# State space layer of a metaformer: decay tiles five turns ahead in eight buffers, one shared copy of B, C and step rows, and the norm's sums, root and scaling four turns later

## Chip, cores and metric

The kernel runs on one core of a Trainium2 chip. The metric is the device time of one execution in microseconds (us). The time before the change is 11213.39 us, the median of 3 runs (11188.75 to 11217.96).

## What is computed

The reference is a network of four layers, each a mixing step and a feed-forward step with residuals. The change touches only the mixing step of the third layer (`L2_conv`), a state space layer (Mamba). Cut to what matters:

```python
x = x + _L2_conv_ref(_ln_c(x), ...)

def _L2_conv_ref(x, ln_g, ln_b, ...):
    xn = (xf - mu) * lax.rsqrt(var + LN_EPS) * ln_g + ln_b      # over d_model
    xm = _mamba(xn, in_proj_w, conv_w, conv_b, x_proj_w, dt_proj_w, dt_proj_b, A_log, D, out_proj_w)
    h1 = gelu(einsum('...w,hw->...h', out, fc1_w) + fc1_b)
    return einsum('...h,oh->...o', h1, fc2_w) + fc2_b

def _mamba(u, ...):
    xi, z = split(einsum('bld,ed->ble', u, in_proj_w))
    xs = silu(causal convolution of xi over l, 4 taps)
    x_dbl = einsum('bld,ed->ble', xs, x_proj_w)
    dt, Bm, Cm = x_dbl[..., :4], x_dbl[..., 4:20], x_dbl[..., 20:]
    dt = softplus(einsum('blr,dr->bld', dt, dt_proj_w) + dt_proj_b)
    A = -exp(A_log)
    def step(h, t):                                   # for every l, 16 states for each of 128 channels
        h = exp(dt_t[:, :, None] * A) * h + (dt_t * x_t)[:, :, None] * B_t[:, None, :]
        y = einsum('bds,bs->bd', h, C_t)
    y = (ys + xs * D) * silu(z)
    return einsum('bld,ed->ble', y, out_proj_w)
```

## The kernel before, in words

The function `l2_conv` does this layer. The sequence is cut into 64 **chunks** of 512 positions for two images each (`b` = 0 and 1). A chunk has 32 **units**, 16 for each image (8 pairs of states times two halves of the channels). One unit sweeps two states of 64 channels as one [128 x 512] tile:

- **decay** (ACT, L2770): `da = exp(dt * A)`, from the tile `dt0` or `dt1` into a tile `da` (5 buffers). It is issued three turns ahead of its unit.
- **spread** (PE, L2780): a matmul that copies the rows of B for two units into a PSUM bank (`bs`); three turns ahead.
- **inputs** (DVE, L2814): `db = dx * bs`, one turn ahead.
- **scan** (DVE, L2822): `hist = scan(da, db)`, the recurrence itself.
- **gs** (POOL, L2827): `hist * C`, with the rows of C fetched by DMA (`cc`); every fourth unit POOL also saves the last column (L2829).
- **summed** (PE, L2838, and L2836 for the term xs * D): adds gs of the states into PSUM, five turns later, two units at a time.

Units 16 and 17 of each chunk are "apart": their da lies in PSUM, and their product is POOL's (L2808).

The order of the work is written by hand. The loop over `t` runs one **turn** per unit; inside a turn every engine gets its instructions in the order decay, spread, fetches, inputs, scan and gs, then the steps that were put down for this turn with `at(turn, ...)`, then summed. The engines take their instructions strictly in this order, so an instruction that waits holds up all that comes later on its engine. Within a turn the steps of `leave` come first, then those of `project`, then those of `norm`.

Four groups of steps feed the units; all turns are counted modulo 32:

- `statistics(n)` serves four chunks at once: DVE takes sums in turns 7 to 22 (L2441), POOL merges them in turn 24 (L2447 to L2453), ACT takes a root in turn 26 (L2457), POOL refines in turn 28 (L2469).
- `norm(n)` prepares the input of a chunk two chunks ahead: `scale` (ACT, L2487, turns 30 and 0), `centre` (PE, L2493, turn 3), `square` (ACT, L2496 and L2497, turn 4), `mean2` (PE, L2502, turn 5), `root` (ACT, L2506 to L2508, turn 6), `newton` (POOL, L2512 to L2515, turn 8), `back` (PE, L2521, turn 11), `kept` (ACT, L2527, turn 12), `done` (POOL, L2534 and L2535, turn 13).
- `project(n)` runs one chunk ahead: the convolution (PE, L2567, turns 24 to 27; ACT, L2579, turn 28), the gate (PE, L2585, turn 30; ACT, L2588), silu (ACT, L2594, turn 1), the rows of B, C and step (PE, L2600, turns 7 and 8), their copies out of PSUM (ACT, L2604 to L2606, turn 9) and corrections for a bf16 remainder (PE, L2615; ACT, L2621; turns 10 to 13), the steps (PE, L2626, turn 15), softplus (ACT, L2630 and L2631 in turn 16, L2634, L2638 and L2639 in turn 17, L2642 in turn 18; POOL, L2645 in turn 18, L2648 in turn 20), `size` (POOL, L2658, turn 21, giving dt) and `scaled` (POOL, L2662, turn 23, giving dx). After each of the last two, SP issues four DMAs (L2654) that lay out dt and dx for the units 0 to 15 of the next chunk; the copies for its other half follow in turns 1 and 2 of that chunk.
- `leave(n)` finishes a chunk: the gating (DVE, L2694, turns 21 and 5), the output product (PE, L2699, turns 9 and 13; ACT, L2702, turns 10 and 14), the two dense layers (PE, L2707, turns 18 and 21; ACT, L2712, turns 19 and 22; GELU, ACT, L2717, turn 24; PE, L2723 to L2726, turns 28 to 32) and the output (ACT, L2733).

In PSUM, the pool `pn` has a single slot for the tiles of centre, mean2, back, the output product and the last layer; `pa` has a single slot for the convolution, the gate, the rows, the steps and the first dense layer. So these follow each other strictly.

The three copies that the change touches are

```python
nc.scalar.copy(tile_of(x_, "bt", [3 * N, 2, L], dt=BF16), ps[0 : 3 * N])
nc.scalar.copy(tile_of(x_, "bc", [2 * N, 2, L], bufs=1), ps[0 : 2 * N])
nc.scalar.copy(tile_of(x_, "r", [R, 2, L], bufs=1), ps[3 * N : 3 * N + R])
```

with N = 32 and R = 4; SP writes `bc[0:N]` to DRAM for the fetches of C, and L2626 multiplies `r` with `dtw`.

Of the kernel before, what the change touches and what calls it, by code (L numbers as in the profile page):

```python
# [10 lines left out]
F32 = mybir.dt.float32  # L11
# [11 lines left out]
P = 128  # L23
# [2278 lines left out]
def l2_conv(env, x, out, prm):  # L2302
# [15 lines left out]
    with ExitStack() as ctx:  # L2318
# [65 lines left out]
        nc.vector.tensor_scalar(minus_i, env.ident[0 : 2 * N, 0 : 2 * N], -1.0, None, ALU.mult)  # L2384
        both = cp.tile([P, H], F32, name="both")
        nc.vector.tensor_add(both, env.ident[:, 0:H], env.ident[:, H:P])
        dtw = load("dtw", [R, D], prm["dt_proj_wT"])
        dtb = load("dtb", [P, 1], prm["dt_proj_b"].unsqueeze(1))
        am = cp.tile([P, S // 2, 2], F32, name="am")
        for i in range(2):  # L2390
# [27 lines left out]
        def at(turn, *steps):  # L2418
            turns.setdefault(turn, []).extend(steps)
# [58 lines left out]
        def norm(n, t0):  # L2478
            g, w0 = chunks[n]
            x_ = boxes[n]  # L2480

            def scale(js):
                r, k = x_["rows"]
                if 0 in js:
                    tile_of(x_, "xn", [P, 3 + L], bufs=3)
                for j in js:
                    nc.scalar.activation(  # L2487
                        x_["xn"][:, 3 + j * C : 3 + j * C + C], r["xt"][:, k + j, :], AF.Identity,
                        bias=r["nb"][:, k + j : k + j + 1], scale=r["rs16"][:, k + j : k + j + 1],
                    )  # L2490

            def centre():
                nc.tensor.matmul(tile_of(x_, "pm", [P, L], "pn", 1, pool=p1), less, x_["xn"][:, 3:], start=True, stop=True)  # L2493

            def square():
                nc.scalar.copy(x_["xn"][:, 3:], x_["pm"])  # L2496
                nc.scalar.activation(tile_of(x_, "sq", [P, L], "sq", 1), x_["pm"], AF.Square)  # L2497

            def mean2():
                pv = tile_of(x_, "pv", [P, NW, 2], "pn", 1, pool=p1)  # L2500
                for q in range(NW):
                    nc.tensor.matmul(pv[:, q, :], x_["sq"][:, q * C : q * C + C], each, start=True, stop=True)  # L2502

            def root():
                v, rs = tile_of(x_, "v", [P, NW, 2]), tile_of(x_, "rs", [P, NW, 2])
                nc.scalar.activation(v, x_["pv"], AF.Identity, bias=env.eps5)  # L2506
                nc.scalar.activation(rs, v, AF.Ln)
                nc.scalar.activation(rs, rs, AF.Exp, scale=-0.5)  # L2508

            def newton():  # L2510
                v, rs, t = x_["v"], x_["rs"], tile_of(x_, "r2", [P, NW, 2])
                nc.gpsimd.tensor_tensor(t, rs, rs, ALU.mult)  # L2512
                nc.gpsimd.tensor_tensor(t, t, v, ALU.mult)
                nc.gpsimd.tensor_scalar(t, t, 0.5, -1.5, ALU.mult, ALU.add)
                nc.gpsimd.tensor_tensor(rs, rs, t, ALU.mult)  # L2515

            def back():
                pr = tile_of(x_, "pr", [P, L], "pn", 1, pool=p1)
                for q in range(NW):
                    for b in range(2):  # L2520
                        nc.tensor.matmul(  # L2521
                            pr[b * H : b * H + H, q * C : q * C + C], x_["rs"][:, q, b : b + 1].to_broadcast([P, H]),
                            env.ident, start=True, stop=True,
                        )

            def kept():
                nc.scalar.copy(tile_of(x_, "rt", [P, L], bufs=1), x_["pr"])  # L2527

            def done():
                xn = x_["xn"]  # L2530
                if w0 == 0:
                    nc.gpsimd.memset(xn[:, 0:3], 0.0)
                else:
                    nc.gpsimd.tensor_copy(xn[:, 0:3], boxes[n - 1]["xn"][:, L : L + 3])  # L2534
                nc.gpsimd.tensor_tensor(xn[:, 3:], xn[:, 3:], x_["rt"], ALU.mult)  # L2535

            at(t0 - 2, lambda: scale((0, 1)))
            at(t0, lambda: scale((2, 3)))
            at(t0 + 3, centre)
            at(t0 + 4, square)  # L2540
            at(t0 + 5, mean2)
            at(t0 + 6, root)
            at(t0 + 8, newton)
            at(t0 + 11, back)
            at(t0 + 12, kept)
            at(t0 + 13, done)


        def project(n, t0):
# [52 lines left out]
            def bcr_out():  # L2602
                ps = x_["ps"]
                nc.scalar.copy(tile_of(x_, "bt", [3 * N, 2, L], dt=BF16), ps[0 : 3 * N])  # L2604
                nc.scalar.copy(tile_of(x_, "bc", [2 * N, 2, L], bufs=1), ps[0 : 2 * N])
                nc.scalar.copy(tile_of(x_, "r", [R, 2, L], bufs=1), ps[3 * N : 3 * N + R])  # L2606

            def c_out():
                for b in range(2):
# [13 lines left out]
            def steps():  # L2623
                pu = tile_of(x_, "pu", [P, 2, L], "pa", 1, pool=pa)
                for b in range(2):
                    nc.tensor.matmul(pu[:, b, :], dtw, x_["r"][:, b, :], start=True, stop=True)  # L2626

            def parts():
                pu = x_["pu"]
# [58 lines left out]
        def leave(n, t0):  # L2688
# [48 lines left out]

            at(t0 - S + LAG, lambda: sums(0))
            at(t0 + LAG, lambda: sums(1))
            at(t0 + 9, lambda: project_out(0))  # L2740
            at(t0 + 10, lambda: projected(0))
            at(t0 + 13, lambda: project_out(1))
            at(t0 + 14, lambda: projected(1))
            at(t0 + 18, lambda: layer1(0))
# [21 lines left out]

        def decay(t):
            x_, b, s, _ = unit(t)
            da = bank(t, t % 2) if apart(t) else sb.tile([P, L], F32, name="da", bufs=5)
            nc.scalar.activation(da, x_["dt%d" % b][:, s % 2, :], AF.Exp, scale=am[:, s : s + 1])  # L2770
            live["da", t] = da

# [72 lines left out]
        with tc.manual_schedule(engines={E_.PE, E_.Activation, E_.DVE, E_.Pool}):  # L2845
            base_table()
            for n in range(0, len(chunks), NG):
                statistics(n, T * (n - 3))
            for n in range(len(chunks)):
                norm(n, T * (n - 2))  # L2850
                project(n, T * (n - 1))
                leave(n, T * (n + 1))
            for t in range(-4 * T, units + 2 * T):
                if 0 <= t + 3 < units:
                    decay(t + 3)
                if 0 <= t + 3 < units:
                    if (t + 3) % 2 == 0 and not apart(t + 3):
                        spread(t + 3)
                if 0 <= t + 10 < units and t % 2 == 0 and apart(t + 10):
                    fetch_b(t + 10)  # L2860
                if 0 <= t + 5 < units and apart(t + 5):
                    inputs_apart(t + 5)
                if t % QU == 2 and 0 <= t + 6 < units:
                    fetch(t + 6)
                if 0 <= t + 1 < units and not apart(t + 1):
                    inputs(t + 1)
                if 0 <= t < units:
                    one_state(t)
                for step in turns.pop(t, ()):
                    step()  # L2870
                if 0 <= t - LAG < units and (t - LAG) % 2 == 1:
                    summed(t - LAG)
# [697 lines left out]
```

## Time and profile before

| | |
|---|---|
| median of 3 runs | 11213.39 us (11188.75 to 11217.96) |
| the profiled execution, own time | 11202.36 us |
| its span, first to last instruction | 11200.5 us |
| the state space layer's units, first to last scan | 6334.0 to 10199.3 us |
| 6330 to 10200 us, busy: DVE, POOL, PE, ACT | 3694.5, 3510.1, 3382.7, 3178.2 of 3870 us |
| granted clock of PE in that stretch | 0.89 |
| mean duration of scan (L2822), input product (L2814) | 1271 ns, 677 ns |
| mean duration of gs (L2827), decay (L2770) | 1273 ns, 715 ns |

A line of the groups reads: line, engine, operation, output and inputs, shapes, count, then busy time and mean ns of one, then the engine's idle time just before these instructions and what ended it. Consecutive instructions of DVE overlap by about 0.1 us, so that a scan and its product take 1.77 us together. A line of the table of waits reads: who waited, for whom, us in total, times, longest. A line of a timeline reads: start, duration, engine, line, operation, operands, and in brackets the idle time before it and what ended it. "PEld" is PE's weight load.

### The profile page before, as it was taken

To read this page: it belongs to the slowest core of one execution; us is meant where nothing else is said; L and a number is where in the kernel's file an instruction comes from. 1 tells how busy PE (TensorE), PEld (TensorE's weight loads), DVE (VectorE), ACT (ScalarE), POOL (GpSimd) and SP (SyncE) were. 2 spreads that over 40 slices of the span, in tenths; PEclk is the share of its full clock that TensorE was granted. 3 is DMA by queue.
4 is the path that set the end of the run, shared out by engine and by line. 5 is a ranking of instruction groups with operands and counts; after the bars stand their busy time and mean duration, and the time that the engine had idled before them with its cause. 6 is when DMAs were issued, how large, how long until landed. Compare 5 with 4: busy or idle time off the path is not lost. (4 is left out here: it accounts for less than half of the span.)

```text
span 11200.5 us, 114412 instructions
## 1 busy us (share of the span) xinstructions
PE 6448.2 (58%) x33010; PEld 3781.1 (34%) x33010; DVE 9431.5 (84%) x14943; ACT 7408.7 (66%) x10451; POOL 5992.4 (54%) x5674
## 2 busy tenths in 40 slices
PE   7777686000000000003999688888888888887665
PEld 5665454000000000002898333333333333334342
DVE  7567646999999999998778599999999999997455
ACT  4244443788886777765555488888888888885443
POOL 1000025899992000001455499999999999894222
PEclk8887798555555555556999789889988989898877
DMA  6312246111111111112111254554554545543534
GB/s 195 107 36 48 56 160 159 51 58 56 59 58 54 57 54 56 53 45 61 47 56 47 70 126 119 127 126 118 131 123 121 128 122 123 129 116 108 193 132 169
DMA packets 806489, 1080.31 MB, mean 96 GB/s; under 512 B 245612, under 2 KB 462927, under 8 KB 792271
## 3 DMA queue, kind: packets, MB, share of 16 engines
q1 hardware_dynamic: 761918, 946.59, 30.6%
q0 software_dynamic: 34368, 124.14, 3.3%
q8 instruction: 266, 4.36, 0.2%
q14 instruction: 385, 3.15, 0.1%
q10 hardware_dynamic: 9552, 2.08, 0.1%
HBM read 699.16 MB, written 255.91 MB: 85 GB/s over the span
## 5 line engine op out<-in xcount | busy, mean ns | idle before, releaser
L2827 POOL TENSOR_TENSOR gs<-hist,cc 128x512 f32<-128x512 f32 x2048 | 2570.8, 1273 | 268.5 <-DVE hist L2822 200.9
L2822 DVE TENSOR_TENSOR_SCAN hist<-da,state,bs 128x512 f32<-128x512 f32 x1860 | 2360.0, 1271 | 48.2 <-ACT da L2770 47.0
L1698 PE MATMUL pm<-ident,m 128*1 128x128 f32 x1 | 0.4, 372 | 3193.0 <-DVE m L1696 3193.0
L2814 DVE TENSOR_TENSOR bs<-dx,bs 128x512 f32<-128x512 f32 x1920 | 1299.3, 677 | 159.9 <-PE bs L2780 110.9
L1506 POOL TENSOR_TENSOR diff<-key 128x2048 f32<-128x2048 f32 (+11 forms) x364 | 1384.0, 3851 | 81.8 <-DVE key L1511 75.5
L2770 ACT ACTIVATE da<-dt,am 128x512 f32<-128x512 f32 x1920 | 1294.5, 715 | 38.2 <-DVE hist L2822 29.7
L2838 PE MATMUL py<-gs,both 128*64 128x512 f32 x4096 | 1212.9, 672 | 1.4 <-POOL gs L2827 1.3
L1698 PEld LDWEIGHTS pm<-ident,m 128*1 128x1 f32 x1 | 0.1, 79 | 3193.1 <-issue 3193.1
L1936 POOL IOTA row<- 72x1 int32 x1 | 0.2, 230 | 1770.4 <-ACTq L1873 1770.4
L1528 ACT COPY keep<-rank 128x1536 int16<-128x1536 int16 (+11 forms) x364 | 612.8, 1686 | 437.7 <-DVE rank L1530 389.0
L1504 ACT COPY low<-key 128x2048 f32<-128x2048 f32 (+11 forms) x364 | 627.7, 1725 | 313.6 <-DVE key L1511 276.5
L1529 DVE COPY_PREDICATED rank<-back,rank 128x1536 int16<-128x1536 uint8 (+11 forms) x364 | 781.7, 2147 | 16.7 <-ACT keep L1528 16.7
L1530 DVE COPY_PREDICATED rank<-back,keep 128x1536 int16<-128x1536 uint8 (+11 forms) x364 | 777.8, 2137 | 12.5
L1511 DVE TENSOR_TENSOR key<-low,key 128x2048 f32<-128x2048 f32 (+11 forms) x364 | 744.5, 2045 | 12.4
L1510 DVE TENSOR_TENSOR key<-low,key 128x2048 f32<-128x2048 f32 (+11 forms) x364 | 749.1, 2058 | 2.4 <-ACT low L1504 2.4
L1507 ACT ACTIVATE turned<-diff 128x2048 int8<-128x2048 f32 (+11 forms) x364 | 600.4, 1699 | 8.4 <-POOL diff L1506 8.4
L1519 ACT ACTIVATE back<-turned 128x3072 uint8<-128x3072 int8 (+12 forms) x182 | 582.5, 3200 | 0.0
L2249 PE MATMUL pe<-ew,xg 128*128 128x128 f32 x4096 | 506.6, 278 | 0.0
L2249 PEld LDWEIGHTS pe<-ew,xg 128*128 128x128 f32 x4096 | 491.0, 193 | 19.2 <-issue 2.9
L1031 POOL DMA_DIRECT2D state<-zz x16 | 18.5, 1156 | 856.2 <-DVE zz L1021 615.8
L2780 PE MATMUL bs<-bt,pick 96*128 96x512 bf16 x960 | 394.5, 411 | 120.0 <-DVE hist L2822 117.5
L2707 PE MATMUL pa<-o,f 128*128 128x256 f32 x1024 | 361.5, 514 | 107.5 <-ACT gl L2712 93.4
(858 smaller groups left out, 17618.0 us busy)
## 6 DMA issues: line engine op xcount, KB each, us to landing
cc<-cd SPq DMA_DIRECT2D x1024, 256.0 KB
xt<-state SPq DMA_DIRECT2D x64, 1024.0 KB
dt<-w SPq DMA_DIRECT2D x512, 128.0 KB
dx<-up SPq DMA_DIRECT2D x512, 128.0 KB
xo<-state SPq DMA_DIRECT2D x128, 256.0 KB
state<-xo POOLq DMA_DIRECT2D x128, 256.0 KB, 3.0
xl<-in_L_ffn_weight SPq DMA_DIRECT2D x32, 1024.0 KB
tk<-in_x SPq DMA_DIRECT2D x32, 512.0 KB
```

Source lines behind the costliest of these rows:

```text
L1504: nc.scalar.copy(c, l)
L1506: nc.gpsimd.tensor_sub(d, lo[part], hi[part])
L1510: nc.vector.tensor_tensor(lo[part], c, hi[part], ALU.min)
L1511: nc.vector.tensor_tensor(hi[part], c, hi[part], ALU.max)
L1529: nc.vector.copy_predicated(l, t, h)
L1530: nc.vector.copy_predicated(h, t, kv)
L2249: T.matmul(w["pe"][:, j, :], w["xg"][:, q, j, :], ew[:, q, :], start=False, stop=(j == 3 and q == E - 1))
L2770: nc.scalar.activation(da, x_["dt%d" % b][:, s % 2, :], AF.Exp, scale=am[:, s : s + 1])
L2814: nc.vector.tensor_mul(live["db", t], x_["dx%d" % b][:, s % 2, :], live["bs", t - s % 2])
L2822: nc.vector.tensor_tensor_scan(h, live.pop(("da", t)), live.pop(("db", t)), 0.0 if first else state[b][:, s : s + 1], ALU.mult, ALU.add,)
L2827: nc.gpsimd.tensor_tensor(gs, h, live.pop(("cc", t)), ALU.mult)
L2838: nc.tensor.matmul(x_["py%d" % b][h * H : h * H + H], both, live.pop(("gs", t - 1 + h)), start=False, stop=(s == S - 1),)
```

## The change

The decay of every unit that is not apart is issued five turns ahead instead of three, and `da` has eight buffers instead of five. The copy `r` is dropped: one copy takes all 100 rows of B, C and step, and the matrix `dtw` becomes [100 x 128], zero but for its last four rows, so that the steps' matmul reads the shared tile with 100 rows instead of 4. In `norm`, square moves by one turn, mean2, root, newton, back and kept by four, done by five. In `leave`, the first output product and its copy move from turns 9 and 10 to 11 and 12.

```diff
-        dtw = load("dtw", [R, D], prm["dt_proj_wT"])
+        dtw = cp.tile([3 * N + R, D], F32, name="dtw")
+        nc.vector.memset(dtw, 0.0)
+        nc.sync.dma_start(dtw[3 * N :], prm["dt_proj_wT"])
...
             at(t0 + 3, centre)
-            at(t0 + 4, square)
-            at(t0 + 5, mean2)
-            at(t0 + 6, root)
-            at(t0 + 8, newton)
-            at(t0 + 11, back)
-            at(t0 + 12, kept)
-            at(t0 + 13, done)
+            at(t0 + 5, square)
+            at(t0 + 9, mean2)
+            at(t0 + 10, root)
+            at(t0 + 12, newton)
+            at(t0 + 15, back)
+            at(t0 + 16, kept)
+            at(t0 + 18, done)
...
-                nc.scalar.copy(tile_of(x_, "bc", [2 * N, 2, L], bufs=1), ps[0 : 2 * N])
-                nc.scalar.copy(tile_of(x_, "r", [R, 2, L], bufs=1), ps[3 * N : 3 * N + R])
+                nc.scalar.copy(tile_of(x_, "bc", [3 * N + R, 2, L], bufs=1), ps[0 : 3 * N + R])
...
-                    nc.tensor.matmul(pu[:, b, :], dtw, x_["r"][:, b, :], start=True, stop=True)
+                    nc.tensor.matmul(pu[:, b, :], dtw, x_["bc"][:, b, :], start=True, stop=True)
...
-            at(t0 + 9, lambda: project_out(0))
-            at(t0 + 10, lambda: projected(0))
+            at(t0 + 11, lambda: project_out(0))
+            at(t0 + 12, lambda: projected(0))
...
-            da = bank(t, t % 2) if apart(t) else sb.tile([P, L], F32, name="da", bufs=5)
+            da = bank(t, t % 2) if apart(t) else sb.tile([P, L], F32, name="da", bufs=8)
...
-                if 0 <= t + 3 < units:
+                if 0 <= t + 5 < units and not apart(t + 5):
+                    decay(t + 5)
+                if 0 <= t + 3 < units and apart(t + 3):
                     decay(t + 3)
```

## The prediction

> **What bounds the kernel now.** I read the page first. Its slices give the state space stage (L2827, L2822, L2814, L2770) to slices 22 to 35, with DVE at nine tenths. The groups name the work: 2048 scans and 1920 input products.
>
> ```profile
> L2822 DVE TENSOR_TENSOR_SCAN hist<-da,state,bs 128x512 f32<-128x512 f32 x1860 | 2360.0, 1271 | 48.2 <-ACT da L2770 47.0
> L2814 DVE TENSOR_TENSOR bs<-dx,bs 128x512 f32<-128x512 f32 x1920 | 1299.3, 677 | 159.9 <-PE bs L2780 110.9 <-DMA dx<-up 46.7
> ```
>
> Their last columns are the idle time that any change can win back: 48 + 111 us, beside one start-up wait of 45.3 us inside the 46.7. The table of waits of the stage (6330 to 10200 us) says what stands behind:
>
> ```profile
> PEld pn L2502 <- ACT sq L2497: 224.7, 61, 5.4
> DVE bs L2814 <- PE bs L2780: 110.9, 100, 3.0
> POOL e L2645 <- ACT less L2639: 65.3, 62, 3.0
> ACT rs L2457 <- POOL v L2453: 65.1, 15, 4.4
> PE pa L2615 <- ACT r L2606: 55.0, 63, 1.7
> DVE hist L2822 <- ACT da L2770: 48.0, 54, 3.1
> ```
>
> Sorting DVE's idle gaps by unit of the chunk (scans counted in order): the da waits lie before unit 5 (40.9 us, of which 32.5 in every fourth chunk, where the statistics of the next four end) and unit 30 (6.1). The waits for PE lie at scans 9 (25.7), 21 (28.4), 25 (41.6) and 1 to 3 (11.3).
>
> The waits that DVE has are half of it. A join that costs nothing yet shows only in the timelines. POOL in one chunk:
>
> ```profile
> 8781.14 1.08 POOL L2535 TENSOR_TENSOR xn<-xn,rt 128x512 f32<-128x512 f32 x1
> ...
> 8788.88 2.36 POOL L2645 TENSOR_TENSOR e<-e,less 128x1024 f32<-128x1024 f32 x1 [0.38 <-ACT less L2639]
> 8791.19 1.27 POOL L2827 TENSOR_TENSOR gs<-hist,cc 128x512 f32<-128x512 f32 x1
> ...
> 8793.77 2.36 POOL L2648 TENSOR_TENSOR up<-up,e 128x1024 f32<-128x1024 f32 x1
> ...
> 8797.31 2.37 POOL L2658 TENSOR_TENSOR w<-w,up 128x1024 f32<-128x1024 f32 x1
> ...
> 8802.22 2.39 POOL L2662 TENSOR_TENSOR up<-w,xs 128x1024 f32<-128x1024 f32 x1
> ```
>
> and DVE, whose line is the next chunk's first product, with no idle before it:
>
> ```profile
> 8809.03 0.67 DVE L2814 TENSOR_TENSOR bs<-dx,bs 128x512 f32<-128x512 f32 x1
> ```
>
> From L2645 to the end of L2662 (8804.61) POOL never rests. Then four DMAs copy dx; the trace's semaphore updates put the last landing 4.15 us later, at 8808.75. DVE starts 0.28 us after that. Over the chunks this slack is mostly 0.2 to 0.6 us (1.2 in the chunk with statistics). So a chunk has two halves, each with its own limit: from the scan of unit 15 to this product (mean of 56 chunks 29.47 us), where POOL's chain is level with DVE, and from there to the next unit 15 (31.08 us), where DVE runs with gaps. 64 x 60.55 = 3875 us, the stage.
>
> **The change, part by part.** The sum is made against the profiled execution: span 11200.5, its own time 11202.4; the median of the runs, 11213.4, is 11 us above.
>
> 1. *Norm's scaling to turn 18.* L2534 and L2535 now follow L2645 on POOL, at the head of the chain above: 1.20 us from start to start (8780.99 to 8782.19). Everything to the landing of dx is late by it. Where they stood, POOL only waited for ACT afterwards (1.0 us a chunk), so nothing comes back. Queued behind them: gs of units 19 to 23, the three big products, SP's copies of dt and dx, and the merge of the statistics (L2453), for which ACT waits.
> 2. *kept (L2527) to turn 16.* It runs behind L2631 and ahead of the decay, L2634, L2638 and L2639, which POOL awaits. Its 0.583 us count as 0.49 between starts. It delays the chain too. Its old place, turn 12, had room.
> 3. *One copy fewer (L2606).* 63 x 1.007 = 63 us leave ACT, and PE's 55 us wait at L2615 goes. Both lie before L2626, and L2626 stands behind the spread of unit 18, which needs scan 14. That start is a floor: 0.3 us after scan 15 begins, reached now in chunks with statistics, against 0.97 in the others. L2626 itself with 100 rows instead of 4: L2567 with 64 rows takes 628 ns, L2600 with 128 rows 680, L2626 652 now: 0 taken, -0.1 to +0.1 us a chunk. The wider copy: 1005 ns for 64 partitions and 1007 for 4, so nothing. The memset and the DMA of dtw stand in the set-up, once, at most one 128x512 DVE product, 0.7 us.
> 4. *Root and sums later (mean2 5 to 9, root 6 to 10, newton, back 11 to 15).* PE's wait at L2502 goes (ACT has four turns for the square), and with it DVE's 25.7 us at scan 9 and a few tenths around it. In its place PE waits for L2694 before L2836 (1.98 us in the last chunk, which has no norm), without a spread behind it that is due. back, 1.09 us, comes after L2626 and hides beside L2630 and L2631 (2.0 us). The output products moved from 9 and 10 to 11 and 12 keep PSUM's single slot in order: one turn between neighbours, as before.
> 5. *Eight da tiles, five turns ahead.* ACT gains two units, 3.5 us, before DVE misses a da: the 48 us of da waits go, the longest being 3.1. The price is the first decay of a chunk, which wants dt two turns sooner. dt lands 4.2 us after L2658, and the third decay behind GELU comes 22.0 us after L2630, so ACT waits some tenths where it has idle time (1 to 1.8 us at L2733 next).
>
> *PE's clock.* With the waits of 3 and 4 gone and back out of the way, PE idles before the spread of unit 18: I add its work from L2836 on (PE free 15.85 us after scan 5, scan 15 at 17.7) and get 1.9 us. The rows show what that can do. Two timelines, 0.32 and 1.34 us of idle time:
>
> ```profile
> 8780.47 0.38 PE L2780 MATMUL bs<-bt,pick 96*128 96x512 bf16 x1 [0.32 <-DVE hist L2822]
> 8780.78 1.98 PE L2626 MATMUL pa<-r,dtw 4*128 4x512 f32 x4
> ```
>
> ```profile
> 9082.44 0.38 PE L2780 MATMUL bs<-bt,pick 96*128 96x512 bf16 x1 [1.34 <-DVE hist L2822]
> 9082.75 3.07 PE L2626 MATMUL pa<-r,dtw 4*128 4x512 f32 x4
> ```
>
> The same four matmuls take 1.98 and 3.07 us; behind 2.1 and 2.8 us of idle time L2630 follows 3.9 us after their start, not 2.1. Of waits between 1 and 2 us some 4 in 10 slow the matmuls behind them. So L2630 starts 0.3 + 2.1 = 2.4 us after scan 15, or 0.3 + 3.5 = 3.8; half and half, 3.1 (now 3.06, and 2.79 with statistics).
>
> [...]
>
> **The sum, a chunk.** Second half: 3.1 + 5.95 (L2630 to the end of L2639) + 0.49 + 0.08 + 2.36 (L2645) + 1.20 + 13.36 (to the end of L2662) + 4.15 = 30.7, +1.2 on 29.47. DVE's gaps at scans 21 and 25 lie inside this half, so what becomes of them no longer matters.
>
> First half: the lowest seen is 28.9, and 30.45 with statistics, mean 29.3. Three chunks in four come down to it but for 0.1 us. In the fourth ACT waits for POOL's merge, now about 1.6 us later against DVE, and PE waits for ACT (L2585, 1.8 to 2.7 us, then 3.4 or more), runs at half pace, and brings the spreads of units 2 and 4 late. One chunk shows it today (PE gap 2.59, DVE's stall 2.95, no da wait), others show the da wait of 3.05 instead. I put 4.6 for what this chunk keeps of its 4.8. Mean 29.3 + (4.6 + 0.3)/4 = 30.5, -0.6.
>
> Together +0.65 x 63 = +41 us: 11202 + 41 = 11243, which is 30 us (0.3%) above the median of the runs.
>
> **Rivals.**
>
> A. *The join does not lengthen much, nothing won beyond it.* PE stays at full pace, L2630 at 2.4: second half 30.0, first 30.5, together as now: 11200, give or take 25. For it: one of the 1.9 us waits in two. Chance 0.30.
>
> B. *Faster.* As A, and the fourth chunk loses its stall too, because DVE, held at the join, gives ACT time: first half 29.4, -1.15 x 63 = -72: 11130. It decides if PE's wait for L2579 stays under about 2 us. Against it: POOL's merge lies behind the same chain. Chance 0.17.
>
> C. *Slower still: PE cold before L2626 in every chunk.* L2630 at 3.8, and the fourth chunk 1 us worse: 31.4 + 30.8, +1.65 x 63 = +104: 11306. It decides from an idle time of about 2 us before the spread of unit 18. Chance 0.13.
>
> D. *The lead of five turns does not arrive,* since dt lands behind the first decay by more than ACT can idle. After L2630, dt lands at 6.44 + 0.08 + 2.36 + 1.20 + 8.45 (L2645's end to L2658's) + 4.2 = 22.7 us, the decay comes at 22.0 + 0.5, so the wait should be 0.2. If it were 2 us and a quarter of that reached DVE, 0.5 x 63 = 32 us came on top: 11275. Chance 0.04.
>
> **How the numbers follow.** Forecast 0.36, A 0.30, B 0.17, C 0.13, D 0.04. The range from 11155 to 11305 leaves out most of B and half of C. About 0.3% (34 us) is what a measurement of this kernel can tell from no change; the forecast lies just over that edge against the profiled time, so I give three quarters of it to slower. Slower is that, C and D (0.27 + 0.17); faster is B and a tenth of A (0.20); the rest, 0.36, is no change.
>
> **What would show it.** Right: the da row of DVE's waits nearly empty; L2502 no longer waits; a new row, DVE L2814 <- DMA dx<-up, some 60 times and 60 to 120 us in all; L2535 directly behind L2645; the stage about 40 us longer. Wrong: no dx row (then POOL's chain was not level with DVE), or the time of L2626's four matmuls at 1.98 us throughout (A), or gaps before units 1 to 5 of each fourth chunk gone (B).

## The result and the profile after

The changed kernel is slower. Its median is 11315.51 us (11260.6 to 11360.3, 6 runs) against 11212.74 us before, a ratio of 1.0092 with a 95% interval of 1.0077 to 1.0107. Slower was forecast, but 11243 us with a range up to 11305; the time lies above it. The profiled execution took 11306.78 us (span 11305.0). Lines 2387 and after have moved by one or two: the scan is L2823, the input product L2815, decay L2771, spread L2781, the steps L2627, softplus L2631 to L2640, mean2 L2504.

The page of the changed kernel answers to the two groups shown of before:

```profile
L2823 DVE TENSOR_TENSOR_SCAN hist<-da,state,bs 128x512 f32<-128x512 f32 x1860 | 2361.8, 1272 | 0.0
L2815 DVE TENSOR_TENSOR bs<-dx,bs 128x512 f32<-128x512 f32 x1920 | 1302.9, 679 | 307.9 <-PE bs L2781 258.6
```

The da waits are gone to the last tenth. DVE's wait for PE's spread has gone from 110.9 to 258.6 us. The table of waits of the stage (6300 to 10350 us; total, times, longest) says what is behind it:

```profile
DVE bs L2815 <- PE bs L2781: 258.6, 140, 3.7
...
PE pa L2708 <- ACT gl L2713: 191.5, 63, 3.3
PEld py L2837 <- DVE y L2695: 181.8, 64, 4.3
ACT e L2631 <- PE pa L2627: 181.2, 62, 4.4
...
ACT rs L2459 <- POOL v L2455: 62.0, 15, 5.6
...
DVE bs L2815 <- DMA dx<-up: 46.5, 9, 39.9
```

Two of these rows stood so in the table of the kernel before (6330 to 10200 us):

```profile
ACT e L2630 <- PE pa L2626: 107.9, 59, 4.2
PE pa L2707 <- ACT gl L2712: 91.7, 54, 2.6
```

Read from below: the dx wait is what it was (39.9 of it is the start-up), so the new wait that was forecast for the join did not come. ACT waits 181 us for the steps (108 before), PE waits 192 us for ACT's L2713 (92 before), and the spreads that stand behind L2708 on PE come late for DVE. Sorted by unit, 161.3 us of DVE's 258.6 lie at scan 25 (41.6 before), 31.0 at scan 19, 18.3 at scan 17, and 47.9 at scans 1 and 3.

POOL's chain has the shape that was forecast, with the scaling directly behind L2646 (its start, duration, line):

```profile
8606.46 2.36 POOL L2646 TENSOR_TENSOR e<-e,less 128x1024 f32<-128x1024 f32 x1 [3.28 <-ACT less L2640]
8608.77 0.18 POOL L2536 COPY xn<-xn 128x3 f32<-128x3 f32 x1
8608.91 1.09 POOL L2537 TENSOR_TENSOR xn<-xn,rt 128x512 f32<-128x512 f32 x1
```

But it begins later: POOL waits 3.28 us for ACT here, 0.38 in the chunk shown of before.

The units take 6328.8 to 10305.8 us, 112 us more. By halves of a chunk (means of 56 chunks, cut as in the prediction):

| us per chunk | before | forecast | after |
|---|---|---|---|
| scan 15 to the next chunk's first product | 29.47 | 30.7 | 31.94 |
| from there to the next scan 15 | 31.08 | 30.5 | 30.58 |
| start of softplus (L2630, now L2631) after scan 15 | 3.02 | 3.1 | 4.54 |

(The first row is the "second half" of a chunk in what follows, the second row the "first half".) The mean of the first half came as forecast. All of the miss is in the second half, and 1.4 us of it stand in the last row.

PE's granted clock in the stage fell from 0.89 to 0.86. Before the change it was low mostly in turns 6 to 8 and 17 to 19; now it is at half pace in turns 11 to 16, in 48 of 56 chunks, and again in turns 22 to 24, behind PE's wait for L2713 (turn 23 is at half pace for 0.94 of the time, 0.52 before). The windows view (time, PE busy, PEclk, DMA share, GB/s), cut on the grid of 3.413 us on which all changes of the clock in this trace lie, shows one chunk from turn 7 to 19:

```profile
8581.46:8584.87 3.41, 3.27 (x12) 1.00 0.42 111
8584.87:8588.28 3.41, 2.59 (x16) 1.00 0.74 187
8588.28:8591.70 3.42, 3.42 (x13) 0.50 0.04 10
8591.70:8595.11 3.41, 3.41 (x12) 0.50 0.41 127
8595.11:8598.52 3.41, 3.41 (x8) 0.50 0.47 104
8598.52:8601.94 3.42, 3.42 (x24) 1.00 0.28 92
```

The second row is the one to look at: PE is busy for 2.59 of 3.41 us, and behind it the clock falls for three windows, over the steps. PE's timeline of that row:

```profile
8584.70 0.38 PE L2781 MATMUL bs<-bt,pick 96*128 96x512 bf16 x1
8584.92 0.95 PE L2504 MATMUL pn<-each,sq 128*128 128x2 f32 x8
8585.80 0.62 PE L2616 MATMUL pa<-bt,minus_i 64*64 64x512 bf16 x2
8586.34 1.08 PE L2839 MATMUL py<-gs,both 128*64 128x512 f32 x4
8588.24 0.58 PE L2781 MATMUL bs<-bt,pick 96*128 96x512 bf16 x1 [0.82 <-DVE hist L2823]
```

0.82 us of idle time alone is less than any fall followed in the two runs below with 100-row steps on the old norm (at least 1.2 us in one, 1.59 in the other). But 0.7 us of the row are mean2's matmuls (L2504), each of two columns. Counted as idle they make it 1.5 us, and so counted no fall in this trace follows less than 1.41 us.

### The profile page after: what moved, and what is told of

It is laid out like the page before. It is cut to its first block, busy times and chain, and to the rows that moved or that the text cites. A ratio compares the mean times of both kernels' runs of the same rounds, so it can differ in the third digit from the quotient of the medians.

```text
span 11305.0 us, 114127 instructions
## 1 busy us (share of the span) xinstructions
PE 6528.0 (58%) x33010; PEld 3869.3 (34%) x33010; DVE 9423.0 (83%) x14944; ACT 7339.8 (65%) x10387; POOL 5998.5 (53%) x5674
## 5 line engine op out<-in xcount | busy, mean ns | idle before, releaser
L2823 DVE TENSOR_TENSOR_SCAN hist<-da,state,bs 128x512 f32<-128x512 f32 x1860 | 2361.8, 1272 | 0.0
L2815 DVE TENSOR_TENSOR bs<-dx,bs 128x512 f32<-128x512 f32 x1920 | 1302.9, 679 | 307.9 <-PE bs L2781 258.6
L2771 ACT ACTIVATE da<-dt,am 128x512 f32<-128x512 f32 x1920 | 1286.3, 716 | 31.9 <-DMA dt<-w 23.0
L2781 PE MATMUL bs<-bt,pick 96*128 96x512 bf16 x960 | 398.7, 415 | 149.8 <-DVE hist L2823 143.5
L2708 PE MATMUL pa<-o,f 128*128 128x256 f32 x1024 | 356.8, 509 | 194.4 <-ACT gl L2713 191.5
```

The costliest lines, as they stand in the source:

```text
L2815: nc.vector.tensor_mul(live["db", t], x_["dx%d" % b][:, s % 2, :], live["bs", t - s % 2])
L2823: nc.vector.tensor_tensor_scan(h, live.pop(("da", t)), live.pop(("db", t)), 0.0 if first else state[b][:, s : s + 1], ALU.mult, ALU.add,)
```

## The experiments

Times are medians; "ratio" is to the kernel before, which ran beside each, with its 95% interval. The kernel before itself had medians from 11201.83 to 11220.28 us in these sets, so what one version costs against another is taken from the ratios here, and given in us as that share of 11213 us. "The copy", "the lead" and "the norm" are the three parts of the change.

**1. One part alone.** The shared copy put on the kernel before:

```diff
-nc.scalar.copy(tile_of(x_, "bc", [2 * N, 2, L], bufs=1), ps[0 : 2 * N])
-nc.scalar.copy(tile_of(x_, "r", [R, 2, L], bufs=1), ps[3 * N : 3 * N + R])
+nc.scalar.copy(tile_of(x_, "bc", [3 * N + R, 2, L], bufs=1), ps[0 : 3 * N + R])
...
-nc.tensor.matmul(pu[:, b, :], dtw, x_["r"][:, b, :], ...)
+nc.tensor.matmul(pu[:, b, :], dtw, x_["bc"][:, b, :], ...)      # dtw with 100 rows
```

> The kernel before with the shared copy of B, C and step rows alone (one ACT copy of 1.0 us fewer per chunk, the steps' matmul with 100 rows). Theory (the lost time comes from norm's move): PE's wait for the dropped copy, 55 us in all, goes, the steps' matmuls start some tenths earlier, and the time is 11190 to 11215. Rival (the wider matmul or copy costs): slower than 11230, with L2626's matmuls above 0.60 us at full clock.

Measured: 11158.80 us, ratio 0.9953 (0.9936 to 0.9969). L2631 starts 2.44 us after scan 15, and the second half is 28.88 us.

The norm (and the output product) alone: all `at(...)` lines of the change in `norm` and `leave`, five da tiles, three copies.

> The kernel before with the moved norm and output product alone, three turns of lead, five da tiles, three copies. Theory (norm's move is the cause: PE's clock falls from turn 11 on, softplus starts 1 to 2 us later, scaling and its copy out of PSUM lengthen the chain to dx by 1.7 us): 11290 to 11350, as the whole change or worse, since the waits for da stay. Rival (the lead of five turns is the cause, ACT's other work falling behind): 11190 to 11220.

Measured: 11316.64 us, ratio 1.0093 (1.0076 to 1.0109). The norm alone costs what the whole change costs, but its trace shows another mix: PE is at half pace in turns 9 to 13 in 22 of 56 chunks only, the steps of 4 rows and what follows them in turns 17 and 18 run at half pace nearly always (0.98 and 0.76 of the time), DVE stalls most at scan 19 (104.2 us, and 36.5 at scan 25), and da waits of 53 us stay. So the two times agree without having one and the same reason. The lead alone was not tried: the author took it that the three more da tiles find room only where the copy drops the tile `r`, which no run shows.

The lead and the copy, with the old norm:

> The changed kernel with norm and output product back at their old turns: eight da tiles, five turns, one copy. Theory: the 48 us of waits for da go, the join with dx (0.3 us of slack) holds back part of it: 11165 to 11195. Rival (the lead is the cause): 11270 or more.

Measured: 11162.47 us, ratio 0.9954 (0.9937 to 0.9970), as the copy alone. No da wait is left, but DVE's wait for PE at scan 9 grows from 23.0 to 75.4 us: the time won at da is spent there, where mean2 waits for ACT's square with the spread behind it.

**2. Is it the chain over POOL?** The changed kernel with one step put back by a turn or two:

```diff
-at(t0 + 18, done)
+at(t0 + 17, done)
```

> The changed kernel with the scaling one turn earlier, in turn 17, ahead of L2645, where POOL waits for ACT. Theory of POOL's chain: its 1.2 us leave the chain, 60 to 75 us less, 11240 to 11260. Theory of PE's clock (softplus starts late and PE's wait for L2713 ahead of the spread of unit 26 sets the second half): within 25 us of the changed kernel, 11290 to 11320, DVE's waits at scan 25 as large as there.

```diff
-at(t0 + 16, kept)
+at(t0 + 17, kept)
```

> The changed kernel with norm's copy out of PSUM (kept) one turn later, behind L2640 instead of ahead of L2635. L2640 ends 0.5 us sooner after L2631. Theory of the chain: 0.5 us a chunk, 30 us less, 11270 to 11285. Theory that PE's wait for L2713 sets the end: L2713 stays where it was, so 11295 to 11320.

And on the version with the lead, the copy and the old norm, `done` alone moved:

```diff
-at(t0 + 13, done)
+at(t0 + 18, done)
```

> Eight da tiles, five turns, one copy; all of norm and the output product at their old turns, but for the scaling on POOL, which stands in turn 18 behind L2645 as in the change. Theory of POOL's chain (the scaling's 1.2 us go into the chain that ends in dx, whose slack is 0.2 to 0.3 us): 1 us a chunk, 60 us, so 11215 to 11235, with DVE waiting for dx in most chunks. Theory of PE's clock (the moved PE work is what costs): no PE work is moved here, so as the kernel without the norm's move, 11155 to 11180.

Measured: 11225.52 us, ratio 1.0025 (1.0014 to 1.0035); 11279.39, 1.0068 (1.0051 to 1.0084); 11167.24, 0.9969 (0.9958 to 0.9981). The second of them, kept one turn later, can't be told from the changed kernel: its interval touches 1.0077 to 1.0107. The scaling's place matters (0.67%), but not by the way that was forecast. With done at 17 the chain to dx is 1.3 us shorter (in three chunks of four L2663, POOL's last product, ends 26.2 instead of 27.5 us after scan 15), and yet the second half stays (31.87 against 31.94 us). What gets shorter is the first half of the fourth chunk, 29.43 instead of 32.43: the merge of the statistics stands behind done on POOL, ACT waits for it (L2459 <- L2455, 42.1 us instead of 62.0), and PE and DVE behind ACT. With the old sums, done at 18 leaves the second half at 28.89 us (28.81 without), and the whole costs 0.15%, with intervals that overlap. (The traced execution with done at 17 took 11263 us, the slowest of nine; so it shows some 44 of the 75 us, and where the rest lies is open.)

Why the longer chain does not count stands in the kernel and in the times at which the DMAs land. Four DMAs lay out dx, half by half, and the product of an even unit reads half 0 alone:

```python
for h in range(2):                    # L2654: half h of dx, two DMAs of 64 rows each
    for i in range(2):
        nc.sync.dma_start(to[i * H : i * H + H, h, :], of[h * H : h * H + H, b, :])
...
nc.vector.tensor_mul(live["db", t], x_["dx%d" % b][:, s % 2, :], live["bs", t - s % 2])
```

So a chunk's first product needs the first two DMAs. In the chunk shown in the prediction the four land 2.25, 2.88, 3.54 and 4.14 us after POOL's end; DVE, at 8809.03, was 0.28 us behind the fourth, but 1.54 us behind the second. Over 56 chunks of the kernel before the second lands 2.9 us after POOL's end and the fourth 4.2 (medians), and in 8 of them DVE starts ahead of the fourth. In the last of the three runs DVE waits at the join in 19 of the 56 chunks: it starts 0.12 to 0.20 us behind the second landing there, and always ahead of the fourth. Before the change it started 4.70 us after POOL's end on average. So there was room for 1.5 us and more in most chunks.

**3. Which turn of the norm costs?** A ladder between the two ends. First the lead, the copy, and the sums moved only a little:

```diff
-at(t0 + 4, square)      -at(t0 + 5, mean2)      -at(t0 + 6, root)      -at(t0 + 8, newton)
+at(t0 + 5, square)      +at(t0 + 7, mean2)      +at(t0 + 8, root)      +at(t0 + 9, newton)
```

with back, kept and done where they were (11, 12, 13).

> Eight da tiles, five turns, one copy, and the short move alone: square in turn 5, the sums in 7, root in 8, newton in 9; back, copy and scaling at 11, 12, 13 and the output product at 9 and 10 as before. The chain behind the softplus is not lengthened, but PE no longer waits for the square. Theory of POOL's chain: 11130 to 11165. Theory of PE's clock (PE, no longer held at the square, runs ahead of DVE, waits in many short pieces and falls to half pace in turns 11 to 17): 11220 or more, softplus starting over 3.5 us after the scan of unit 15.

Then back, kept and done as in the change:

```diff
-at(t0 + 11, back)      -at(t0 + 12, kept)      -at(t0 + 13, done)
+at(t0 + 15, back)      +at(t0 + 16, kept)      +at(t0 + 18, done)
```

> The version with the early sums (square 5, mean2 7, root 8, newton 9; 11085 us), with back, kept and done at 15, 16 and 18 as in the changed kernel; the output product stays at 9 and 10. It parts the late scaling from the late sums. Pace theory (what costs is PE's half pace in turns 11 to 16, which begins where PE has run out of work ahead of the spread of unit 12; back's 1.1 us leaves turn 11): 11130 to 11200, and the half pace appears in turns 12 to 16 in part of the chunks. Chain theory (kept on ACT and done on POOL, 0.49 and 1.20 us ahead of the chain to dx, and the merge of the statistics behind it; measured as 17 us for done alone and 27 us for kept from 16 to 17): 11085 + 17 + 27 + some 50 for the merge = 11130 to 11180, without half pace in turns 11 to 16. Sums theory (the sums at 9 to 12 are what costs): under 11120.

Then the output product as well; what is left to the changed kernel are the sums at 9, 10 and 12:

```diff
-at(t0 + 9, lambda: project_out(0))       -at(t0 + 10, lambda: projected(0))
+at(t0 + 11, lambda: project_out(0))      +at(t0 + 12, lambda: projected(0))
```

> The same with the first output product moved from turns 9 and 10 to 11 and 12 as well: what is left to the changed kernel is the sums alone (square 5, mean2 7, root 8, newton 9 in place of 5, 9, 10, 12). Pace theory: the output product is what fed PE before the spread of unit 12; with it gone from there, 11240 to 11310 and half pace in turns 11 to 16 as in the changed kernel. Chain theory: the output product is not in the chain, so as the run with the late scaling alone, within 20 us. Sums theory: under 11130, and the step to 11315 comes with the sums.

| step | us | ratio | second half | first half |
|---|---|---|---|---|
| lead, copy, sums at 7 to 9 | 11085.02 | 0.9892 (0.9876 to 0.9909) | 29.04 | 29.72 |
| + back, kept, done late | 11230.8 | 1.0017 (1.0006 to 1.0028) | 29.97 | 31.03 |
| + output product late | 11232.45 | 1.0020 (1.0009 to 1.0030) | 30.29 | 30.66 |
| + sums at 9 to 12 (the change) | 11315.51 | 1.0092 (1.0077 to 1.0107) | 31.94 | 30.58 |

None of the theories had it whole. The late tail costs 1.25% (140 us), 1.3 of its 2.2 us a chunk in the first half; there ACT waits 70.6 us for the merge (48.2 in the version above), and one step further on PE waits for ACT at the gate, 50.2 us in all (26.1 in the version above):

```profile
PE pa L2587 <- ACT xs L2581: 50.2, 17, 4.6
```

The output product costs nothing. The late sums cost 0.72% (81 us), all in the second half, together with the early half pace: 48 of 56 chunks have 1 us or more of it in turns 9 to 13, and 12 of 56 in the row above, whose mean2 runs in turn 7.

The trace of the changed kernel says the same within one execution. In its 48 chunks with that half pace softplus starts 4.86 us after scan 15 and the second half takes 32.39 us; in the other eight it is 2.59 and 29.25 us, less than before the change, though kept and done stand late in them too.

The first version of the ladder beats both kernels. DVE's wait for the spread, 258.6 us in the changed kernel, is down to this:

```profile
DVE bs L2815 <- PE bs L2781: 58.6, 64, 2.5
```

Two runs take it apart: the little move alone, and with the copy but without the lead.

> The kernel before with the sums moved a little and nothing else (square 4 to 5, mean2 5 to 7, root 6 to 8, newton 8 to 9; back, kept and done old; five da tiles, three copies). If the wait for the square is worth what it seemed (70 us between the versions with and without it), 11130 to 11160; if it pays only where the copy has gone, since ACT then has the time, 11190 to 11220.

> The same with the shared copy, without the eight da tiles: the difference to the version with all three (11085) is what the lead of five turns is worth once PE's wait for the square is gone. If the lead is worth something there, since the da waits (46 us) no longer move to scan 9: 11110 to 11135. If it is worth nothing, as beside the old norm: 11075 to 11095.

Measured: 11208.95 us, ratio 0.9996 (0.9987 to 1.0005), and 11148.75, 0.9945 (0.9931 to 0.9959). Alone the move wins nothing that can be measured, beside the copy hardly more (0.08%, with intervals that overlap), beside copy and lead 0.62% (70 us). And the lead, worth nothing with the old norm (0.9954 against 0.9953), is worth 0.53% (59 us) here: its da waits (49.1 us at unit 5) do not come back as a stall at scan 9, since PE no longer waits for the square.

**4. Why does PE run at half pace?** The changed kernel with PE's idle time filled: the second product of the rows, and mean2's matmuls, made twice.

```diff
-nc.tensor.matmul(x_["ps"][0 : 3 * N + R, b, :], xp, x_["xs"][:, b, :], start=True, stop=True)
+for _ in range(1 + b):
+    nc.tensor.matmul(x_["ps"][0 : 3 * N + R, b, :], xp, x_["xs"][:, b, :], start=True, stop=True)
...
-for q in range(NW):
+for q in (*range(NW), *range(NW)):
     nc.tensor.matmul(pv[:, q, :], x_["sq"][:, q * C : q * C + C], each, start=True, stop=True)
```

> The changed kernel with more work for PE and the same results: the second of the two matmuls for B, C and step rows (turn 8) and the four of the norm's sums (turn 9) run twice, some 2 us a chunk, in the time in which PE now waits for DVE before the spreads of units 12 and 14. Theory (PE's clock): with the idle time filled the matmuls of turns 11 to 15 keep full pace, the steps' four take 2.0 us, softplus starts 2.5 to 3.1 us after the scan of unit 15 (4.5 in the changed kernel), and the time falls by 50 to 100 us to 11210 to 11260, although PE does 64 x 2 us more. Rival (the lengthened chain on POOL alone sets the end): 11300 to 11330, no gain from it.

Measured: 11329.75 us, ratio 1.0097 (1.0080 to 1.0114): no help. PE's waits in turns 9 to 11 were gone (0.90 to 0.03 us a chunk), and the clock fell all the same in 48 of 56 chunks; softplus started even later, 5.41 us after scan 15. So idle time as the profile shows it did not decide here. I then sorted all windows of 3.41 us (56 chunks) in which the clock was full by whether it fell at their end, once by PE's idle time and once with mean2's matmuls (two columns) and, where they have 4 rows, those of the steps counted as idle:

| kernel | falls | with under 1.2 us idle | the same, small matmuls counted as idle | most idle, clock kept |
|---|---|---|---|---|
| before | 132 | 41 | 0 | 1.78 |
| after | 119 | 42 | 0 | 1.79 |
| doubled small matmuls | 131 | 39 | 0 | 1.79 |
| copy alone (steps of 100 rows) | 103 | 0 | 0 | 1.90 |

Before the change, many of these falls follow a window without any idle time, with the steps in it (the same views of one chunk):

```profile
8541.44 1.98 PE L2626 MATMUL pa<-r,dtw 4*128 4x512 f32 x4
```

```profile
8540.78:8544.19 3.41, 3.41 (x11) 1.00 0.24 59
8544.19:8547.60 3.41, 2.80 (x8) 0.50 0.48 139
```

That suggests that these small matmuls act as idle time does in this kernel; three runs test it. The filling of the run above with one dense matmul in place of mean2's second time, for the same added time of PE (0.86 us a chunk):

```diff
-pv = tile_of(x_, "pv", [P, NW, 2], "pn", 1, pool=p1)
+pv = tile_of(x_, "pw", [P, L], "pn", 1, pool=p1)
+nc.tensor.matmul(pv, less, x_["xn"][:, 3:], start=True, stop=True)
+pv = x_["pv"] = pv[:, 0 : 2 * NW].rearrange("p (q two) -> p q two", two=2)
```

> The changed kernel with PE's work filled as in the run with doubled matmuls (11330 us, no help), but with one dense matmul of 128 columns by 512 ahead of mean2's small ones, in place of making these twice; the second rows product is made twice, as there. The added PE time is the same (0.86 and 0.86 us a chunk). Work theory: in that run the windows of turns 9 and 10 held 1.6 us and more of small matmuls and idle time; here the idle time is filled with dense work and only mean2's own 0.9 us counts as idle, so the half pace of turns 11 to 16 goes in most chunks and L2631 comes 1 to 1.5 us earlier: 11190 to 11260. Idle theory (only time without any matmul counts): no different from small ones, 11300 to 11335.

Measured: 11232.59 us, ratio 1.0013 (1.0004 to 1.0022), 0.8% below the changed kernel though PE does more work. 1 us or more of half pace in turns 9 to 13 is left in 6 of 56 chunks (48 without), softplus starts 2.89 us after scan 15 (4.54), and the second half takes 29.86 us (31.94), in an execution of 11210 us, the fastest of eleven. The windows at the same place of a chunk:

```profile
8539.62:8543.03 3.41, 3.41 (x11) 1.00 0.65 171
8543.03:8546.45 3.42, 3.42 (x18) 1.00 0.41 93
8546.45:8549.86 3.41, 3.41 (x24) 1.00 0.10 34
8549.86:8553.27 3.41, 3.37 (x13) 1.00 0.85 197
```

Then the steps' rows, parted from ACT's time: three copies as before, but the steps multiplied with 100 rows; and one copy fewer, but the steps with 4 rows, which a DMA takes from the shared copy.

```diff
-nc.scalar.copy(tile_of(x_, "bc", [2 * N, 2, L], bufs=1), ps[0 : 2 * N])
+nc.scalar.copy(tile_of(x_, "bc", [3 * N + R, 2, L], bufs=1), ps[0 : 3 * N + R])
 nc.scalar.copy(tile_of(x_, "r", [R, 2, L], bufs=1), ps[3 * N : 3 * N + R])
...
-nc.tensor.matmul(pu[:, b, :], dtw, x_["r"][:, b, :], ...)
+nc.tensor.matmul(pu[:, b, :], dtw, x_["bc"][:, b, :], ...)
```

> The kernel before, with the steps multiplied from the shared copy of 100 rows and a dtw of 100 rows, but with all three copies still made by ACT (the small one, r, is written and never read). So ACT's time is the old one, and only the steps' matmuls have 100 rows in place of 4. Work theory (a matmul of few rows or columns counts as idle time for the clock): the falls of the clock behind the four-row matmuls go, 41 of 132 in the stage, the times of turns 17 to 19 come back to full pace, and most of the shared copy's 53 us is here: 11165 to 11195. ACT theory (the copy pays since ACT and PE's wait at the corrections get 1 us back): 11205 to 11225.

```diff
-nc.scalar.copy(tile_of(x_, "bc", [2 * N, 2, L], bufs=1), ps[0 : 2 * N])
-nc.scalar.copy(tile_of(x_, "r", [R, 2, L], bufs=1), ps[3 * N : 3 * N + R])
+nc.scalar.copy(tile_of(x_, "bc", [3 * N + R, 2, L], bufs=1), ps[0 : 3 * N + R])
+nc.sync.dma_start(tile_of(x_, "r", [R, 2, L], bufs=1), x_["bc"][3 * N :])
```

> The kernel before, with one copy of 100 rows in place of two, and the four rows r taken from it by a DMA of SP's, so that ACT's time is that of the shared copy and the steps' matmuls keep 4 rows. The DMA has five turns (9 us) to land. ACT theory: as the shared copy, 11150 to 11170. Work theory: 11185 to 11220, with falls of the clock behind the steps' matmuls as before.

Measured: with 100 rows 11209.17 us, ratio 0.9980 (0.9971 to 0.9989), and no fall behind less than 1.59 us of idle time in 109 falls; with 4 rows and the copy gone 11181.79, 0.9963 (0.9950 to 0.9977), with 41 of 138 falls behind less than 1.2 us again, none of them when the steps' matmuls count as idle. So it holds in these runs, but by these medians the rows are the smaller part in this place: of the copy's 0.47%, 0.37% is there without the rows, and 0.20% with the rows alone (with intervals of 0.1 to 0.2% either way). The work theory had priced that the other way round.

Last, real dense work in place of a filling: the version of 11085 us with the two products of the rows at turns 5 and 6 instead of 7 and 8, ahead of the matmul that waits 1.9 us for DVE's y.

```diff
-at(t0 + 7, lambda: bcr(0))
-at(t0 + 8, lambda: bcr(1))
+at(t0 + 5, lambda: bcr(0))
+at(t0 + 6, lambda: bcr(1))
```

> The fastest version so far (11085 us: da tiles, shared copy, sums moved a little) with the two products of the rows of B, C and step moved from turns 7 and 8 to 5 and 6, ahead of the matmul that waits 1.9 us for DVE's y. It fills that wait with 1.7 us of dense work. Work theory: the half pace of turns 6 to 8 (half of the chunks) goes, but the time won there lets PE run dry later, before the spread of unit 10 or 12, and nothing there is awaited: 11065 to 11090. Idle theory: the same. A rival for both: PE gets to mean2 before ACT's square is done and waits there with the spread of unit 10 behind it: over 11110.

Measured: 11156.28 us, ratio 0.9940 (0.9926 to 0.9953), 0.5% worse. The time is the rival's, the reason is not: there is no wait at scan 9. The half pace of turns 6 to 8 goes and comes back in turns 9 to 13 (PE idles 1.3 us more in turns 7 and 8), with the steps and the spreads of units 18 and 26 behind it in the chunk after the statistics (softplus 5.83 us after scan 15 there, 2.26 without). An idle stretch was moved from where nothing was due to where something was.

## Why the prediction failed

- **The sign was right, and so was the mean of the first half:** -0.50 us a chunk was measured, -0.6 forecast. Part of that is luck. Two chunks of four came to 29.0 us, as forecast. The chunk after the statistics was to keep nearly all of its stall, at 33.5 us, and took 32.4: 30.2 to 30.4 in seven of fourteen cases, 33.0 to 36.1 in the others. The chunk with the statistics was put at 30.5 and took 31.9. The two misses cancel. The da waits and the stall at scan 9 went, and PE's new wait for y (L2695, 1.9 us in turn 5) made nothing late directly. The wait for dt stayed at tenths (23.0 us in all, 20 of them in the start-up).
- **The term that was mis-sized: L2630's start, put at 3.1 us after scan 15, measured 4.54.** It carries 1.4 us x 63 = 91 us; what was missing is (1.98 - 0.65) x 63 = 84 us of the stage (a chunk took 62.52 us, 60.54 before). The step behind it is "PE's clock". It looked for idle time in one place, before the spread of unit 18, and took 2.4 and 3.8 us "half and half". The 1.9 us of idle time that it worked out there did come, but only in the eight chunks at full pace (1.2 to 2.3 us in turns 13 to 15); in the other 48 PE, at half pace since turn 11, had none, and softplus came at 4.86 us. The step moved mean2 from turn 5 to 9 and counted only its wait; it didn't ask what mean2's eight matmuls are to the clock. In the chunk shown they take 0.95 us in turn 9 and end 1.6 us before an idle stretch of 0.82 us, and the window that holds both has 1.5 us, with 1.41 the least that a fall followed in that trace. The run with dense matmuls shows this cause for the late sums.
- **The share of "4 in 10" for idle times of 1 to 2 us was a mixture** of two things that the trace lets one part: where the windows of 3.413 us lie (a wait cut in two by their border did nothing: behind 1.18 and 1.34 us in neighbouring windows of the changed kernel the clock stayed full), and small matmuls beside the wait. The slow L2626 that the prediction showed, behind 1.34 us of idle time, was itself such a matmul, of 4 rows: 0.7 us of it lay in the same window, which makes 2.0.
- **"Everything to the landing of dx is late by it" was true and did not matter, since POOL's chain was not "level with DVE".** The prediction measured the slack of "0.2 to 0.6 us" from the last of the four landings, 4.15 us after POOL's end. The product needs the second, and to that the slack was mostly 1.5 to 1.8 us (2.4 to 2.5 in the chunk with statistics). So 1.2 us of scaling fitted in, and moving done back by a turn left the second half where it was.
- **That the rest of the sum for the second half came out is luck.** From L2645 to the end of L2662 16.92 us were forecast and 16.90 measured. But POOL ended 27.9 us after scan 15, so that half 0 of dx was there at about 30.9, and DVE came at 31.94: the last term, 4.15 us, stood in for DVE's own stalls. What sets that half is the step which the prediction put aside: "DVE's gaps at scans 21 and 25 lie inside this half, so what becomes of them no longer matters". 161 us of DVE's stalls are at scan 25.
- **The scaling does cost, elsewhere:** through the merge of the statistics behind it, which the prediction named and put at "about 1.6 us later" in one chunk of four. One turn earlier is worth 0.67%.
- **"0 taken" for 100 rows missed an effect:** the duration at full pace hardly moves (587 ns with 4 rows before, 592 with 100 in the changed kernel), but in the run with 100 rows alone no fall follows less than 1.59 us of idle time (before, 32 falls follow none at all), and the time falls by 0.20%. The copy's own term (L2630 from 3.06 to 2.4) was right: 2.44.
- **The lead was priced at what its waits were, 48 us.** They went, and their time with them, into the next wait on the same path (scan 9), unless the square's wait goes too.
- **Rival C** (11306, PE cold in every chunk) came nearest, and its idea was the right one in 48 of 56 chunks; its place and the point at which it decides were not.

Not settled: the late tail (1.25%) was moved as one piece. The traces put 1.3 of its 2.2 us a chunk to the first half, where the merge is late, and the rest to kept's 0.49 us and to some half pace in turns 15 to 17; no run parts these. Nor is it known how far the output product (64 columns) counts for the clock: in two runs (the little move alone, and the rows at turns 5 and 6) 23 and 8 falls are explained only if it counts as idle too. And each version was traced in one execution, while the six times of the changed kernel spread over 100 us; the traces do not say what sets these apart.

## What to carry to other kernels

When a step is moved on TensorE, look at what its matmuls are and not only at how long they take: in this kernel eight two-column matmuls (0.95 us) in one window with a wait of 0.82 us were followed by half the clock for three windows, 10.2 us, and four-row ones by half the clock behind a window without any wait (PE busy for 3.41 of 3.41 us). Put such groups where a slow stretch hurts nobody, here beside the wait in turns 5 to 8, and keep what is due soon out of the windows behind them. Price a removed wait together with the next one on its path: three edits that won 0.47% (the copy), 0.08% (the little move beside it) and nothing (the lead beside it) won 1.08% together. And where several transfers fill a tile, take the slack from the one that the reader needs first, not from the last.

## What the runs showed of the hardware

- In the traces of the kernels before and after, all changes of TensorE's granted clock lie on a grid of 3.413 us, to 0.02 us; in the state space stage stretches of half pace last one to three steps of it before the change and one to four after it (3.4 to 13.7 us).
- With mean2's matmuls (128x2), and those of the steps where they have 4 rows (4x512), counted as idle, every fall before the change (132 in 56 chunks) follows a window with 1.51 us or more, and every fall after it (119) one with 1.41 us or more; the most that a window held behind which the clock stayed full was 1.78 and 1.79 us, so between these it went either way. The clock came back behind windows with at most 0.32 us of idle time before the change and 0.53 after it.
- By the profile alone, which has these matmuls as busy, 41 of the 132 falls before the change follow less than 1.2 us of idle time, 32 of them none at all, and 42 of the 119 after it. With steps of 100 rows (100x512) on the kernel before, all 109 falls follow 1.59 us or more. With one dense matmul in place of mean2's second time, 6 of 56 chunks have 1 us or more of half pace in turns 9 to 13, against 48.
- Of the four DMAs of 128 KB that lay out dx, SP issues one about every 0.6 us; the second lands 2.9 us and the fourth 4.2 us after the end of the product that they copy (medians of 56 chunks before the change), at most 4.4 and 6.2.
